# ScalarE in place of VectorE: the first layer's statistics and both FFNs' normalization

## The chip, the core and the metric

The kernel runs on one NeuronCore of one Trainium2 chip. The core has TensorE (PE; PEld are its weight loads), VectorE (DVE), ScalarE (ACT), GpSimd (POOL) and SyncE (SP), each with a queue of instructions that it works off in order; 16 DMA engines move data. The metric is the device time of one execution in microseconds (us), as a median of several. A profile is one further execution, recorded by the hardware profiler.

## The reference

The input x has 16 batches of 512 tokens with 256 features, in float32. Four layers are applied, each on a normalized copy of x (mean 0, variance 1 over the 256 features, no learned factors), and each added to x:

```python
x = x + mamba(layernorm(x))        # a recurrence over the 512 tokens, 16 states per feature
x = x + ffn(layernorm(x))          # "f"
x = x + attention(layernorm(x))    # "a": linear attention, 16 heads of 16
x = x + ffn(layernorm(x))          # "g", same weights as f

def layernorm(x, eps=1e-05):
    m = mean(x, axis=-1); v = var(x, axis=-1)
    return (x - m) / sqrt(v + eps)

def ffn(x): return fp4_linear(silu(fp4_linear(x, w_gate)) * fp4_linear(x, w_up), w_down)
```

`fp4_linear` rounds both of its operands to a 4-bit grid in blocks of 16 along the last dimension, with one scale per block, before it multiplies. The hidden width is 704. Only the two FFNs need the normalized x itself, since it is rounded. In the other two layers the mean is taken out of the weights beforehand, and 1/sqrt(v + eps) is applied while x is transposed.

## The kernel before

**Tiles.** A batch of x stays in one SBUF tile `x` of 128 partitions by 4 chunks by 256 features: a partition holds one token of each chunk. All steps on features are written chunk by chunk, four times per batch.

**Statistics.** There are two ways to get them. The first layer (`front`, lines 435 to 447) uses VectorE: for each chunk `bn_stats` (L442) and `bn_aggr` (L443) give mean and variance, of which only the variance is used. The later layers take the sum of x as a by-product of the residual addition (`residual`, L377, or the halves at L571 added up at L578). `distances` (L384) then lets ScalarE compute the squares of (sum - 256 x), and the accumulator of that instruction gives their sum over the features; the squares themselves go to a scratch tile `squares` that nobody reads. `summed` allots the two small tiles of 128x4, sums and distances, under tags with a number and two buffers each: 0 for f, 1 for g, 2 for a. `inverse` scales the variance and adds epsilon on VectorE (L392) and raises it to the power -0.5 on GpSimd (L394): this gives `rstd`, 128x4, with a tag number of its own (2 for the first layer, 3 for a, 0 and 1 for the FFNs).

**Normalization.** `layernorm` (lines 397 to 409), called by `ffn` alone, calls `inverse`, divides the sums by 256 on VectorE (L402), and then normalizes each chunk by one VectorE instruction (L405) that subtracts the mean and multiplies by rstd, both operands of one value per partition. Its tile `xn` has one buffer per FFN. `fp4` follows on the whole tile of 1024 values per partition: block maxima (L230, `amax`), `half`, `inv`, a product (L244, `v`), an absolute value on ScalarE (L248, `big`), two VectorE instructions that round (L250, L251), and a last product back into `xn` (L252). The tile is then transposed for the matmuls (L418).

**First layer.** `prologue` goes on from `front`: `to_features` lets ScalarE make a diagonal matrix of rstd (L424, `diag_m`) and TensorE multiply x by it (L426), which transposes and scales at once. After projections the scan begins (`mamba`): 16 steps per batch. In each, a DMA spreads the step sizes over the partitions into one of four `bar` buffers (L520), ScalarE makes the decays (L527 exponential, twice, and L530 square), VectorE scans (L548) and multiplies (L552), and TensorE sums up (L558).

**FFN.** For each chunk TensorE computes gate and up (L605), ScalarE a tanh (L611), VectorE two products (L612, L613), and after another `fp4` TensorE transposes (L627), ScalarE copies to SBUF (L631, L636) and TensorE multiplies by w_down (L640).

**Order.** Each stage is a Python generator: it issues some instructions and yields a number, about the microseconds that this piece is to count. `run_all` (from L865 on) starts four stages per batch b, the scan at b, f at b+1.0, attention at b+2.1 and g at b+3.1, and always lets the stage go on that stands earliest. A stage advances by yield times length over total, and the totals are a line of constants:

```python
    SCAN, FFN, ATTN = 65.7, 40.2, 25.7
```

So a scan of batch b runs beside f of b-1, attention of b-2 and g of b-3. Within the scan of batch b, `weave` mixes in the prologue of batch b+1, one piece of it after each scan step from the second on. The yields in `front` are 2.4 after the statistics and 1 after `to_features`; in `ffn` 2.2 follows `layernorm` and 7 follows its `fp4`. The order in which the code issues instructions gives them their priority. The framework's scheduler settles each engine's queue when the kernel is built, and an instruction whose operands come early may stand ahead of ones that were issued before it: in the trace, the `bn_stats` of batches 1 to 4 start at 19, 53, 55 and 57 us, and the first scan step at 62 us.

Of the kernel before, what the change touches and what calls it, by code (L numbers as in the profile page):

```python
# [10 lines left out]
F32 = mybir.dt.float32  # L11
BF16 = mybir.dt.bfloat16
AF = mybir.ActivationFunctionType
ALU = mybir.AluOpType
# [3 lines left out]
P = 128  # L18
# [14 lines left out]
def kernel(  # L33
# [18 lines left out]
    nc = tc.nc  # L52
    B, S, D = x.shape
# [5 lines left out]
    NC = S // P  # L59
# [27 lines left out]
    small = ctx.enter_context(tc.tile_pool(name="small", bufs=2))  # L87
# [9 lines left out]
    begun, turned, stats, halfway = {}, {}, {}, [0]  # L97
# [21 lines left out]
    squares = const.tile([P, D], BF16, name="squares")  # L119
# [248 lines left out]
    def summed(i, name):  # L368

        sums = small.tile([P, NC], F32, tag=f"sum{i}", name=f"sum_{name}")  # L370
        dist = small.tile([P, NC], F32, tag=f"dist{i}", name=f"dist_{name}")
        return sums, dist
# [10 lines left out]
    def distances(xt, c, sums, dist):  # L383
        nc.scalar.activation(  # L384
            squares, xt[:, c, :], AF.Square, bias=sums[:, c : c + 1], scale=-float(D),
            accum_out=dist[:, c : c + 1],
        )

    def inverse(i, var, by, name):

        shifted = small.tile([P, NC], F32, tag=f"var{i}", name=f"var_{name}")
        nc.vector.tensor_scalar(shifted, var, by, LN_EPS, ALU.mult, ALU.add)  # L392
        rstd = small.tile([P, NC], F32, tag=f"rstd{i}", name=f"rstd_{name}")
        nc.gpsimd.tensor_tensor(rstd, shifted, neg_half, ALU.pow)  # L394
        return rstd

    def layernorm(i, xt, stats, name):

        sums, dist = stats
        rstd = inverse(i, dist, 1.0 / D**3, name)  # L400
        mean = small.tile([P, NC], F32, tag=f"mean{i}", name=f"mean_{name}")
        nc.vector.tensor_scalar(mean, sums, 1.0 / D, None, ALU.mult)  # L402
        xn = acts[i].tile([P, NC, D], F32, tag="xn", name=f"xn_{name}", bufs=1)
        for c in range(NC):
            nc.vector.tensor_scalar(  # L405
                xn[:, c, :], xt[:, c, :], mean[:, c : c + 1], rstd[:, c : c + 1],
                ALU.subtract, ALU.mult,
            )
        return xn

    def to_features(pool, t, name, rstd=None):

        tT = pool.tile([P, ND, S], F32, tag="tT", name=f"tT_{name}", bufs=1)
        if rstd is None:
            for k in range(ND):
                pt = bank(f"pt_{name}_{k}")
                for c in range(NC):
                    nc.tensor.transpose(pt[:, ts(c, P)], t[:, c, ts(k, P)], ident)  # L418
                nc.scalar.copy(tT[:, k, :], pt)
            return tT  # L420
        pts = [bank(f"pt_{name}_{k}") for k in range(ND)]
        for c in range(NC):
            diag = small.tile([P, P], F32, tag="diag", name=f"diag_{name}_{c}")
            nc.scalar.activation(diag, ident, AF.Copy, scale=rstd[:, c : c + 1])  # L424
            for k in range(ND):
                nc.tensor.matmul(  # L426
                    pts[k][:, ts(c, P)], t[:, c, ts(k, P)], diag, start=True, stop=True
                )
        for k in range(ND):
            nc.scalar.copy(tT[:, k, :], pts[k])  # L430
        return tT
# [2 lines left out]

    def front(b, xt):

        stats = small.tile(
            [P, NC, nc.vector.BN_STATS_DIM], F32, tag="stats", name=f"st_m{b}"
        )
        mv = small.tile([P, NC, nc.vector.BN_AGGR_DIM], F32, tag="mv", name=f"mv_m{b}")  # L440
        for c in range(NC):
            nc.vector.bn_stats(stats[:, c, :], xt[:, c, :])  # L442
            nc.vector.bn_aggr(mv[:, c, :], stats[:, c, :])  # L443
        rstd = inverse(2, mv[:, :, 1], 1.0, f"m{b}")
        yield 2.4
        turned[b] = to_features(one, xt, f"m{b}", rstd)
        yield 1

    def prologue(b, xt):

        yield from front(b, xt)
        xnT = turned.pop(b)

# [129 lines left out]
    def ffn(i, nm, b, xs):  # L583
        xt = xs[b]
        act = acts[i]
        xq = layernorm(i, xt, stats.pop((nm, b)), f"{nm}{b}")
        if i == 0:
            stats["a", b] = summed(2, f"a{b}")
# [271 lines left out]
        nc.sync.dma_start(out[b].rearrange("(c p) d -> p c d", p=P), xs[b])  # L860


    SCAN, FFN, ATTN = 65.7, 40.2, 25.7

    def run_all(stages):  # L865

# [62 lines left out]
```

## Time and profile before

| | |
|---|---|
| runs | 2825.38 us median of 3 (2824.58 to 2828.75) |
| the profiled execution, its own time | 2823.49 us |
| its span, first to last instruction | 2821.8 us |
| mean granted TensorE clock | 0.942 of full |
| HBM traffic | 146.02 MB read, 16.78 MB written, 58 GB/s over the span |
| from 500 to 2480 us | PE busy 1779.00, DVE 1786.84, ACT 1093.81 of 1980.00 us |
| from 2480 us to the end | PE busy 287.32, DVE 211.69, ACT 96.24 of 341.80 us |

How to read the profile's lines: an instruction group has its line in the kernel, its engine and operation, the tile it writes and those it reads (`out<-in`, buffer numbers left out; the letter at the end of a name is the layer: m first layer, f and g the FFNs, a attention), the shapes as partitions by elements, and how often it occurred. In the rows by form there follow the busy time in us and the mean duration of one in ns, then the idle time of the engine just before, in us, and what ended it. In a timeline the first number is the start in us from the span's start, the second how long the row took, and brackets give idle time before it and who ended it; instructions of the same kind in a row are merged and counted with x. Durations of neighbours on an engine overlap somewhat. In the table by stretch of time each engine has its busy time and the number of instructions, in the order PE, PEld, DVE, ACT, POOL, and at the end the granted clock, the DMA share and GB/s. The chain of waits is followed back from the last instruction, at each step to what released it.

Here is how the same two stages stand in the whole: VectorE executes 64 `bn_stats`, 64 `bn_aggr`, 32 means and 128 normalizations in an execution; ScalarE executes 192 squares with accumulators.

### The profile page before, as it was taken

The page shows a single profiled execution, that of the slowest core. Times are in us where ns is not written, and L with a number is a line of the kernel's source. Part 1 is how long each engine was busy: PE and PEld are TensorE (multiplying, and loading weights), DVE is VectorE, ACT ScalarE, POOL GpSimd, SP SyncE. Part 2 cuts the span into 40 slices and gives each one's busy share as a digit, 9 for nine tenths or more (in the row PEclk, how much of TensorE's full clock was granted, in tenths as well). Part 3 has the DMA queues.
Part 4 walks back from the last instruction along what each step waited for, and adds up shares of the span by engine and source line. Part 5 has one row for each costly group of instructions (what it writes and reads, how often), then busy time and mean ns, then how long its engine had stood idle before and what let it go on. Part 6 is the DMA issues. An engine that isn't in the chain of part 4 may idle for free.

```text
span 2821.8 us, 34272 instructions
## 1 busy us (share of the span) xinstructions
PE 2449.7 (87%) x12907; PEld 1441.9 (51%) x12907; DVE 2430.5 (86%) x3689; ACT 1492.1 (53%) x2846; POOL 172.2 (6%) x171
## 2 busy tenths in 40 slices
PE   5677989799898989989898998989899898889886
PEld 3234545455555555555555555555555554556564
DVE  7898888898999898899989889998988999868465
ACT  4776564465646455464645556464555646333321
POOL 2000000000000010000001000000100000000000
PEclk7788999899999999999999999999999999999897
DMA  5533212222223131322313132131213213000000
GB/s 142 131 93 82 64 49 53 67 53 83 52 60 76 38 75 45 82 53 54 82 38 75 45 82 53 47 89 38 75 45 83 53 45 82 24 8 1 8 8 8
DMA packets 97146, 165.01 MB, mean 58 GB/s; under 512 B 8434, under 2 KB 92372, under 8 KB 96980
## 3 DMA queue, kind: packets, MB, share of 16 engines
q1 hardware_dynamic: 95360, 161.77, 22.3%
q8 instruction: 101, 1.65, 0.3%
q10 hardware_dynamic: 1620, 1.06, 0.1%
q14 instruction: 65, 0.53, 0.1%
HBM read 146.02 MB, written 16.78 MB: 58 GB/s over the span
## 4 chain that ended last, share of the span: by engine, by line
DVE 40%; PE 36%; DMA 9%; ACT 9%; issue 3%; POOL 2%; SPq 0%; POOLq 0%; ACTq 0%; DVEq 0%
DVE h L548 15%; DMA bar<-dd 9%; PE pg_g L605 5%; DVE h L552 4%; PE pu_g L605 4%; PE po_g L640 4%; PE pg_f L605 3%; PE pu_f L605 3%; PE py L558 3%; ACT bar L527 2%; PE pz L457 2%; DVE v_f L244 2%; DVE sm L729 2%; PE pqk L678 2%; ACT bar L530 1%
## 5 line engine op out<-in xcount | busy, mean ns | idle before, releaser
L548 DVE TENSOR_TENSOR_SCAN h<-bar,inp 128x1024 f32<-128x1024 f32 x256 | 579.4, 2277 | 13.9 <-PE py L558 7.6
L527 ACT ACTIVATE bar<-bar,a_col 128x511 f32<-128x511 f32 x512 | 352.4, 715 | 339.6 <-DMA bar<-dd 291.5
L558 PE MATMUL py<-h,red 128*32 128x512 f32 x1024 | 288.7, 645 | 119.3 <-DVE h L552 118.2
L552 DVE TENSOR_TENSOR h<-h,cm 128x1024 f32<-128x1024 f32 x256 | 311.1, 1218 | 0.6
L530 ACT ACTIVATE bar<-bar 128x1022 f32<-128x1022 f32 x256 | 269.3, 1052 | 3.0
L640 PE MATMUL po_g<-wdT,hqT_g 128*128 128x256 f32 (+1 forms) x768 | 214.3, 425 | 41.8 <-ACT hqT_g L631 41.8
L640 PEld LDWEIGHTS po_g<-wdT,hqT_g 128*128 128x128 f32 (+1 forms) x768 | 149.0, 206 | 120.3 <-ACT hqT_g L631 65.1
L640 PE MATMUL po_f<-wdT,hqT_f 128*128 128x256 f32 (+1 forms) x768 | 198.2, 400 | 9.6 <-ACT hqT_f L631 9.6
L605 PE MATMUL pg_g<-wgT,tT_g 128*128 128x352 f32 x512 | 190.7, 492 | 0.3 <-DVE sm L729 0.3
L640 PEld LDWEIGHTS po_f<-wdT,hqT_f 128*128 128x128 f32 (+1 forms) x768 | 137.5, 192 | 94.6 <-ACT hqT_f L636 29.0
L605 PE MATMUL pu_g<-wuT,tT_g 128*128 128x352 f32 x512 | 182.3, 480 | 0.0
L605 PE MATMUL pg_f<-wgT,tT_f 128*128 128x352 f32 x512 | 181.8, 478 | 0.0
L605 PE MATMUL pu_f<-wuT,tT_f 128*128 128x352 f32 x512 | 172.7, 460 | 3.4 <-DVE sm L729 3.0
L729 DVE TENSOR_TENSOR sm<-psc,causal 128x512 f32<-128x512 f32 x256 | 163.9, 681 | 10.8 <-PE psc L722 5.9
L611 ACT ACTIVATE h_g<-pg_g 128x352 f32<-128x352 f32 x128 | 59.1, 462 | 195.3 <-PE pg_g L605 195.1
L558 PEld LDWEIGHTS py<-h,red 128*32 128x32 f32 x1024 | 37.8, 110 | 221.6 <-DVE h L552 171.4
L605 PEld LDWEIGHTS pu_g<-wuT,tT_g 128*128 128x128 f32 x512 | 103.3, 202 | 60.7 <-issue 11.4
L763 POOL COPY dx<-den 128x256 f32<-128x256 f32 x64 | 42.2, 660 | 1482.7 <-PE pr L768 795.5
L248 ACT ACTIVATE big_f<-v_f 128x704 bf16<-128x704 f32 (+1 forms) x80 | 67.2, 840 | 122.3 <-DVE v_f L244 122.3
L605 PEld LDWEIGHTS pg_f<-wgT,tT_f 128*128 128x128 f32 x512 | 96.3, 196 | 66.9 <-issue 23.2
L612 DVE SCALAR_TENSOR_TENSOR h_g<-h_g,pg_g 128x352 f32<-128x352 f32 x128 | 65.5, 512 | 74.2 <-ACT h_g L611 72.8
L678 PE MATMUL pqk<-tT_a,w_qkv_sb 128*128 128x512 f32 x256 | 121.6, 614 | 7.4 <-ACT tT_a L430 7.4
(237 smaller groups left out, 4707.0 us busy)
## 6 DMA issues: line engine op xcount, KB each, us to landing
bar<-dd SPq DMA_DIRECT2D x256, 511.0 KB, 4.7
x<-in_L_attn_a_x_dram SPq DMA_DIRECT2D x16, 512.0 KB, 4.5
dd<-dt SPq DMA_DIRECT2D x128, 64.0 KB, 1.7
out_dram<-x SPq DMA_DIRECT2D x16, 512.0 KB, 4.4
w_qkv_sb<-in_L_attn_b_W_attn_dram ACTq DMA_DIRECT2D x1, 768.0 KB, 7.1
raw_d<-in_L_ffn_w_down_dram SPq DMA_DIRECT2D x1, 704.0 KB
raw_g<-in_L_ffn_w_gate_dram SPq DMA_DIRECT2D x1, 640.0 KB, 7.1
raw_u<-in_L_ffn_w_up_dram SPq DMA_DIRECT2D x1, 640.0 KB, 6.5
```

Of the source, the lines that this page charges most:

```text
L248: nc.scalar.activation(big, v, AF.Abs, scale=STEP)
L527: nc.scalar.activation(bar[:, i, 1:S], bar[:, i, 1:S], AF.Exp, scale=a_col[:, g : g + 1])
L530: nc.scalar.activation(bar[:, :, 1:S], bar[:, :, 1:S], AF.Square)
L548: nc.vector.tensor_tensor_scan(h.rearrange("p i t -> p (i t)"), bar.rearrange("p i t -> p (i t)"), inp.rearrange("p i t -> p (i t)"), 0.0, ...
L552: nc.vector.tensor_tensor(h, h, cm.unsqueeze(1).to_broadcast([P, 2, S]), ALU.mult)
L558: nc.tensor.matmul(py[32 * q : 32 * q + 32, :], red[:, j, :], (h0, h)[q // 2][:, q % 2, :], start=False, stop=(j == 3),)
L605: nc.tensor.matmul(pw[:, :HF], xqT[:, k, ts(c, P)], wT[:, k, cols], start=(k == 0), stop=(k == ND - 1),)
L611: nc.scalar.activation(hc, pg[:, :HF], AF.Tanh, scale=0.5)
L612: nc.vector.scalar_tensor_tensor(hc, hc, 1.0, pg[:, :HF], ALU.add, ALU.mult)
L640: nc.tensor.matmul(po[:, :D], hqT[:rows, r, :], wdT[:rows, r, :], start=(r == 0), stop=(r == NR - 1),)
L678: nc.tensor.matmul(pz, w_qkv_sb[:, k, ts(je, P)], xnT[:, k, :], start=(k == 0), stop=(k == ND - 1),)
L729: nc.vector.tensor_tensor(t, psc[g].rearrange("p (s t) -> p s t", t=P), causal.unsqueeze(1).to_broadcast([P, NH // 4, P]), ALU.mult,)
```

## The change

In `layernorm` the VectorE instruction for the mean becomes one for a shift, -mean times rstd, which needs rstd. The four VectorE normalizations become four ScalarE activations of the function Identity, which compute x times scale plus bias, with rstd as scale and the shift as bias. In `front` the eight VectorE instructions for statistics become eight on ScalarE: for each chunk a Copy whose accumulator gives the sum, and `distances`, which reads that sum. Both write their full result to `squares`. The small tiles come from `summed(0, ...)`, whose two tags the first FFN also uses. The yield after the statistics is 0.2 in place of 2.4, and the scan's total is 63.5 in place of 65.7. The yields and the total of the FFN stay.

```diff
@@ layernorm
         rstd = inverse(i, dist, 1.0 / D**3, name)
-        mean = small.tile([P, NC], F32, tag=f"mean{i}", name=f"mean_{name}")
-        nc.vector.tensor_scalar(mean, sums, 1.0 / D, None, ALU.mult)
+        shift = small.tile([P, NC], F32, tag=f"mean{i}", name=f"shift_{name}")
+        nc.vector.scalar_tensor_tensor(shift, sums, -1.0 / D, rstd, ALU.mult, ALU.mult)
         xn = acts[i].tile([P, NC, D], F32, tag="xn", name=f"xn_{name}", bufs=1)
         for c in range(NC):
-            nc.vector.tensor_scalar(
-                xn[:, c, :], xt[:, c, :], mean[:, c : c + 1], rstd[:, c : c + 1],
-                ALU.subtract, ALU.mult,
+            nc.scalar.activation(
+                xn[:, c, :], xt[:, c, :], AF.Identity, bias=shift[:, c : c + 1],
+                scale=rstd[:, c : c + 1],
             )
@@ front
-        stats = small.tile(
-            [P, NC, nc.vector.BN_STATS_DIM], F32, tag="stats", name=f"st_m{b}"
-        )
-        mv = small.tile([P, NC, nc.vector.BN_AGGR_DIM], F32, tag="mv", name=f"mv_m{b}")
+        sums, dist = summed(0, f"m{b}")
         for c in range(NC):
-            nc.vector.bn_stats(stats[:, c, :], xt[:, c, :])
-            nc.vector.bn_aggr(mv[:, c, :], stats[:, c, :])
-        rstd = inverse(2, mv[:, :, 1], 1.0, f"m{b}")
-        yield 2.4
+            nc.scalar.activation(squares, xt[:, c, :], AF.Copy, accum_out=sums[:, c : c + 1])
+            distances(xt, c, sums, dist)
+        rstd = inverse(2, dist, 1.0 / D**3, f"m{b}")
+        yield 0.2
         turned[b] = to_features(one, xt, f"m{b}", rstd)
         yield 1
@@ the stages' totals
-    SCAN, FFN, ATTN = 65.7, 40.2, 25.7
+    SCAN, FFN, ATTN = 63.5, 40.2, 25.7
```

## The prediction, made before the change was run

> **What bounds the kernel now.** I read the page's shares first, then busy time by stretch, then the timelines of VectorE (DVE) and ScalarE (ACT) where the moved steps sit, then the rows by form. From the page:
>
> ```profile
> PE 2449.7 (87%) x12907; PEld 1441.9 (51%) x12907; DVE 2430.5 (86%) x3689; ACT 1492.1 (53%) x2846; POOL 172.2 (6%) x171
> ...
> DVE 40%; PE 36%; DMA 9%; ACT 9%; issue 3%; POOL 2%; SPq 0%; POOLq 0%; ACTq 0%; DVEq 0%
> ```
>
> Two engines are nearly full, and neither carries the end alone: 40% of the span is followed back to VectorE, 36% to TensorE, 9% to ScalarE. Busy time by stretch (columns: PE, PEld, DVE, ACT, POOL):
>
> ```profile
> 1037.00:1044.00 7.00, 6.91 (x30) 3.97 (x30) 7.00 (x13) 4.93 (x16) 1.35 (x1) 1.00 0.33 85
> 1044.00:1052.00 8.00, 4.01 (x17) 2.25 (x14) 7.29 (x21) 6.98 (x14) 2.90 (x3) 1.00 0.25 57
> 1052.00:1060.00 8.00, 7.42 (x25) 3.77 (x24) 8.00 (x8) 3.16 (x8) 0.58 (x1) 0.79 0.12 34
> ```
>
> The timelines repeat every 165 us per batch from the fourth batch on: four VectorE normalizations in a row start at 880.27, 1044.60 and 1209.89. A batch's head, some 33 us from 1037 on, holds the first FFN's normalization, the second FFN's (of an older batch) and the attention's start together. There VectorE is full (32.25 of 33 us), but from 1044 to 1052 ScalarE is at 6.98 of 8 too. VectorE, then ScalarE, in that stretch one batch later:
>
> ```profile
> 1209.89 1.38 DVE L405 TENSOR_SCALAR xn_f<-x,mean_f,rstd_f 128x256 f32<-128x256 f32 x4 [0.56 <-POOL rstd_f L394]
> ...
> 1211.33 1.21 DVE L230 TENSOR_REDUCE amax_f<-xn_f 128x64 f32<-128x1024 f32 x1
> ...
> 1217.26 1.22 DVE L250 SCALAR_TENSOR_TENSOR v_f<-big_f,v_f 128x1024 f32<-128x1024 bf16 x1 [0.26 <-ACT big_f L248]
> ```
>
> ```profile
> 1210.23 1.33 ACT L527 ACTIVATE bar<-bar,a_col 128x511 f32<-128x511 f32 x2
> 1212.43 0.72 ACT L527 ACTIVATE bar<-bar,a_col 128x511 f32<-128x511 f32 x1 [0.86 <-DMA bar<-dd]
> ...
> 1216.19 1.04 ACT L248 ACTIVATE big_f<-v_f 128x1024 bf16<-128x1024 f32 x1
> ```
>
> VectorE goes from normalizing straight to the block maximum, and is already kept waiting (0.26 us here, 0.51 in another batch) by ScalarE's `big_f`. So the moved work leaves a full engine for one that is nearly full just there.
>
> **What VectorE loses.** Rows by form:
>
> ```profile
> L384 ACT ACTIVATE squares<-x,sum_g 128x256 bf16<-128x256 f32 x64 | 32.3, 505 | 21.8 <-DVE x L377 20.8
> L715 ACT ACTIVATE ko<-qk,odd_heads 128x256 f32<-128x256 f32 x64 | 30.8, 501 | 25.3 <-DVE qk L686 21.5 <-PE psc L722 3.8
> L442 DVE BATCH_NORM_STATS2 st_m<-x 128x6 f32<-128x256 f32 x64 | 24.3, 398 | 0.1
> L405 DVE TENSOR_SCALAR xn_g<-x,mean_g,rstd_g 128x256 f32<-128x256 f32 x64 | 24.2, 392 | 3.7 <-POOL rstd_g L394 3.7
> ```
>
> Instructions overlap, so a duration overstates what an engine gets back. Four normalizations take 1.38 us with a last one of 0.41: one per (1.38-0.41)/3 = 0.323 us. Eight per batch: 2.6 us; 128 in all: 41 us. Two bn_stats in a row take 0.71 us with one of 0.39, so 0.32 each, and their bn_aggr adds 0.09 before the next starts (1020.57 to 1020.65): 0.41 per pair, 1.65 us per batch, 26 us in all. Together 4.25 us per batch, 67 us. The shift replaces the mean at the same size (128x4): L402 takes 0.14 to 0.17 us; I take no difference, bounded by 0 and +0.1 us, as it multiplies by a second operand. The variance step on 128x4 stays. Busy time falls by more, as durations count there: 46.7 (L405) + 24.3 + 10.1 = 81 us, to about 2350.
>
> **What ScalarE gains.** The squares of one batch start 0.635 us apart (1203.76, 1204.39, 1205.03), read-out of the accumulator included. The new Copy with a sum has no row; bounds are 0.46 (a plain 256-wide copy of 0.37 plus 0.09 for the read-out's tail) and 0.635 (the square). I take 0.56, nearer the square, which also reads SBUF and its accumulator. [...] So (0.56+0.635+0.03)x4 = 4.9 us per batch (4.4 to 5.2). For an Identity with both scale and bias per partition the trace has no row: L715 (scale) and L384 (bias) have one such operand and take 0.50. [...] I take 0.49: 2.06 us for four (1.7 to 2.4), 4.1 per batch. ScalarE gains 9.0 us per batch, 144 us in all; its busy time goes to about 1640. No activation table is added that I can see: Copy and Square already run among the others without a load beside them, and Identity, which is not in the trace, costs 1.28 us per load if it is otherwise (the L472 load's row), up to twice per normalization.
>
> [...]
>
> **Where it lies on the path.** First the statistics. At 1019 to 1022 bn_stats are followed by this VectorE row:
>
> ```profile
> 1027.25 0.52 DVE L612 SCALAR_TENSOR_TENSOR h_f<-h_f,pg_f 128x352 f32<-128x352 f32 x1 [3.53 <-ACT h_f L611]
> ```
>
> VectorE idles until ScalarE has done a tanh, which comes after decays that waited for a transfer. Taking 1.65 us away ahead of that wait gains about nothing there. ScalarE's 4.9 us burst is emitted before the fourth step's decay, and ScalarE stood still there for 4.18 us, waiting on that DMA. If it goes into that hole it costs about 0.2 us (what sticks out, less slack); behind the wait it would push the tanh by up to 4.9. The first result is needed 35 us later (var_m at 1022.4, `diag_m` at 1057), so the variance's and POOL's power's delay is hidden. For batch 0 the power on POOL runs only at 18.5 us, behind its other powers; five microseconds on ScalarE are hidden by that. If batch 0's rstd came late, it would cost up to 3 us once. The yield from 2.4 to 0.2 and SCAN from 65.7 to 63.5 let the rest of the prologue be issued earlier against the other stages, by 2.2/65.7 of 165 us = 5 us; issue order, no work. I value it at zero, bounded by -0.5 and +1 us per batch, since a changed order can change every wait of the period.
>
> The normalizations: VectorE saves 2.6 us per batch where it is full. Against it: (1) the shift waits for POOL as the first normalization did (0.56), but then `amax_f` waits 0.16 + 2.06 + hand-overs, some 2.3 us. Behind it VectorE has the g variance, a residual (0.34) and a scan product (1.14), about 1.6 us, ready: 0.7 uncovered. (2) `xn_g` is covered by f's maximum, reciprocal and product (2.7 us). (3) 4.1 us on ScalarE come ahead of `big_f`: 1209.9 to 1217.2 is 7.3 us with 0.86 idle, so `big_f` ends 3.3 us later; VectorE by then has removed 2.6 us but can bring forward `amax_g`, `half_g`, `inv_g` and a scan (4.0 us). Between 0 and 3.2 us remain; I take 0.7, nearer zero, as the order on a queue is already not the order of the code (bn_stats of batches 1 to 4 run before the first scan). Per batch: -2.6 + 0.7 + 0.7 + 0.2 = -1.0 us; thirteen batches have both in full stretches: -13. Four normalizations (f of batch 15, g of 13, 14, 15) stand in the tail, where VectorE has 212 of 342 us and waits: 1.38 becomes 0.16+2.06+0.2, +1.0 each: +4. Sum -9 us.
>
> A check by shares: VectorE's 40% of 2822 us over 2430 busy is 0.46 us of span per us; ScalarE's 9% over 1492 is 0.17. -67x0.46 + 144x0.17 = -31 + 24 = -7. The two agree. From the profiled execution, 2823.5 (span 2821.8), I get 2814.5; it lies 1.9 below the median of the runs, so 2816.
>
> **Rivals.**
> 1. VectorE's whole saving counts: -67x0.85 (the share outside start and tail) + 4 = -53: 2772. For it: VectorE full in the heads. Against: 36% of the chain is TensorE's, whose work stays. Chance 0.10.
> 2. Slower: ScalarE late at `big_f` in the batch head. If VectorE's order leaves nothing before `v_f` L250, it waits 3.2 us instead of 0.7: +1.5 per batch, x13 + 4 = +24: 2849. It decides from 1.7 us of added wait on. For it: ScalarE at 6.98 of 8 and VectorE already waiting; against: 4 us of movable work. Chance 0.40, the disturbed issue order included.
> 3. Nothing reaches the end, TensorE or bar transfers take the relief: 2825. Chance 0.12.
>
> **How the numbers follow.** A small gain (0.38; own range 2795 to 2819) and rival 1 make 0.48 for faster by over 0.2% (5.7 us, about what a measurement of this kernel can tell from no change), 0.12 within, 0.40 slower. The range reaches up past rival 2 to 2858 and down near rival 1, to 2778.
>
> **What would show it.** DVE near 2350 and ACT near 1640 busy; the period between normalizations 164 us; `amax_f` waiting for ScalarE's `xn_f` under 1 us, `v_f` L250 for `big_f` about 1 us. A wait of over 1.7 us there, or `h_f` waits above 3.5 us, would make rival 2 right. New table loads, or a normalization of over 2.4 us, would make the prices wrong; so would a period that changes while those waits stay.

## The result, and the profile after

The changed kernel takes 2866.34 us in the median of 4 runs (2859.41 to 2869.59), the kernel before 2826.86 (4 runs, 2824.58 to 2828.75): a ratio of 1.0137, 95% interval 1.0116 to 1.0158. It is slower by 39 us, where 9 us of gain were predicted, and lies outside of the predicted range of 2778 to 2858. The profiled execution took 2865.66 us, its span is 2863.9, its mean granted TensorE clock 0.929 (before: 0.942).

From the page after, shares of the engines and then the chain that ended last:

```profile
PE 2442.8 (85%) x12907; PEld 1449.6 (51%) x12907; DVE 2369.5 (83%) x3433; ACT 1600.3 (56%) x3230; POOL 194.3 (7%) x171
...
PE 31%; DVE 30%; ACT 21%; DMA 10%; POOL 4%; issue 4%; SPq 0%; POOLq 0%; ACTq 0%; DVEq 0%
```

VectorE lost 61 us of busy time and ScalarE got 108, yet VectorE's share fell from 86 to 83% of a longer span: it is more often idle. Lines behind 445 have numbers 3 lower than before. The rows by form of what was moved, and of the waits behind it (busy, mean ns of one, idle before and its releaser):

```profile
L405 ACT ACTIVATE xn_f<-x,shift_f,rstd_f 128x256 f32<-128x256 f32 x64 | 33.3, 590 | 15.1 <-DVE shift_f L402 15.1
...
L439 ACT ACTIVATE squares<-x 128x256 bf16<-128x256 f32 x64 | 25.8, 403 | 1.1 <-DMA x<-in_L_attn_a_x_dram 1.0
...
L250 DVE SCALAR_TENSOR_TENSOR v_f<-big_f,v_f 128x1024 f32<-128x1024 bf16 x16 | 19.5, 1219 | 11.5 <-ACT big_f L248 11.5
L230 DVE TENSOR_REDUCE amax_f<-xn_f 128x64 f32<-128x1024 f32 x16 | 19.4, 1215 | 0.6 <-ACT xn_f L405 0.4
...
L402 DVE SCALAR_TENSOR_TENSOR shift_f<-sum_f,rstd_f 128x4 f32<-128x4 f32 x16 | 2.6, 163 | 14.5 <-POOL rstd_f L394 14.5
```

One Identity with two operands takes 590 ns, four in a row 2.07 us (2.06 predicted). The two waits that the prediction watched are small: `amax_f` waited 0.4 us for ScalarE in all, `v_f` 11.5/16 = 0.7 us per batch. The head of a batch before, and then the changed kernel's: GpSimd's power of f and VectorE's rows behind it, and then ScalarE's:

```profile
1042.65 1.91 POOL L394 TENSOR_TENSOR rstd_f<-var_f,neg_half 128x4 f32<-128x4 f32 x1 [13.79 <-DVE var_f L392]
...
1046.04 1.21 DVE L230 TENSOR_REDUCE amax_f<-xn_f 128x64 f32<-128x1024 f32 x1
```

```profile
1063.10 1.91 POOL L394 TENSOR_TENSOR rstd_f<-var_f,neg_half 128x4 f32<-128x4 f32 x1 [15.20 <-DVE var_f L392]
...
1065.05 0.17 DVE L402 SCALAR_TENSOR_TENSOR shift_f<-sum_f,rstd_f 128x4 f32<-128x4 f32 x1 [0.90 <-POOL rstd_f L394]
...
1065.19 2.29 DVE L545 TENSOR_TENSOR_SCAN h<-bar,inp 128x1024 f32<-128x1024 f32 x1
1068.31 0.16 DVE L402 SCALAR_TENSOR_TENSOR shift_g<-sum_g,rstd_g 128x4 f32<-128x4 f32 x1 [0.83 <-POOL rstd_g L394]
1068.39 2.28 DVE L545 TENSOR_TENSOR_SCAN h<-bar,inp 128x1024 f32<-128x1024 f32 x1
...
1070.92 1.21 DVE L230 TENSOR_REDUCE amax_f<-xn_f 128x64 f32<-128x1024 f32 x1
```

```profile
1065.24 2.07 ACT L405 ACTIVATE xn_f<-x,shift_f,rstd_f 128x256 f32<-128x256 f32 x4 [0.60 <-DVE shift_f L402]
...
1073.08 0.40 ACT L439 ACTIVATE squares<-x 128x256 bf16<-128x256 f32 x1
...
1078.96 1.04 ACT L248 ACTIVATE big_f<-v_f 128x1024 bf16<-128x1024 f32 x1
```

`amax_f` need not wait, since two whole scans stand ahead of it: it starts 7.8 us after GpSimd's power of f, before 3.4. And the first layer's statistics, which were to fill a hole near 1019, run at 1073 to 1081, in this head.

From the fifth power of f to the fifteenth, f recurs every 170.3 us; before, every 165.0: these ten periods lose 53 us. The stretch ahead of them loses 11 more (724.5 against 713.4 us), and the stretch behind them wins 22 back (437 against 459 us, 5 of it after the last scan): 42 us of span in all. So most of the loss is the 5.3 us of each steady period, and the question is what in the period carries it.

### The profile page after: what moved, and what is told of

Its sections match the earlier page's. It is cut to its first block, busy times and chain, and to the rows that moved or that the text cites. A ratio compares the mean times of both kernels' runs of the same rounds, so it can differ in the third digit from the quotient of the medians.

```text
span 2863.9 us, 34409 instructions
## 1 busy us (share of the span) xinstructions
PE 2442.8 (85%) x12907; PEld 1449.6 (51%) x12907; DVE 2369.5 (83%) x3433; ACT 1600.3 (56%) x3230; POOL 194.3 (7%) x171
## 4 chain that ended last, share of the span: by engine, by line
PE 31%; DVE 30%; ACT 21%; DMA 10%; POOL 4%; issue 4%; SPq 0%; POOLq 0%; ACTq 0%; DVEq 0%
DVE h L545 13%; DMA bar<-dd 10%; PE po_g L637 7%; ACT bar L524 4%; ACT bar L527 3%; PE pg_g L602 3%; PE py L555 3%; PE pu_g L602 3%; DVE h L549 2%; PE pg_f L602 2%; PE pu_f L602 2%; POOL rstd_g L394 1%; ACT big_f L248 1%; DVE amax_f L230 1%; PE pn L750 1%
## 5 line engine op out<-in xcount | busy, mean ns | idle before, releaser
L555 PE MATMUL py<-h,red 128*32 128x512 f32 x1024 | 262.7, 658 | 148.6 <-DVE h L549 148.5
L637 PE MATMUL po_g<-wdT,hqT_g 128*128 128x256 f32 (+1 forms) x768 | 248.1, 477 | 81.2 <-ACT hqT_g L628 81.2
L637 PEld LDWEIGHTS po_g<-wdT,hqT_g 128*128 128x128 f32 (+1 forms) x768 | 171.1, 236 | 178.0 <-ACT hqT_g L628 113.6
L637 PE MATMUL po_f<-wdT,hqT_f 128*128 128x256 f32 (+1 forms) x768 | 197.7, 399 | 14.7 <-ACT hqT_f L628 14.7
L602 PE MATMUL pg_g<-wgT,tT_g 128*128 128x352 f32 x512 | 183.8, 482 | 11.4 <-ACT dt L464 7.5
L726 DVE TENSOR_TENSOR sm<-psc,causal 128x512 f32<-128x512 f32 x256 | 163.9, 682 | 28.7 <-PE pn L750 22.7
L555 PEld LDWEIGHTS py<-h,red 128*32 128x32 f32 x1024 | 34.7, 111 | 254.3 <-DVE h L549 208.1
L760 POOL COPY dx<-den 128x256 f32<-128x256 f32 x64 | 32.1, 502 | 1778.5 <-PE pr L765 1236.7
L609 DVE SCALAR_TENSOR_TENSOR h_f<-h_f,pg_f 128x352 f32<-128x352 f32 x128 | 65.7, 514 | 86.6 <-ACT h_f L608 86.6
L602 PEld LDWEIGHTS pu_f<-wuT,tT_f 128*128 128x128 f32 x512 | 97.0, 191 | 61.6 <-DVE x L377 8.4
```

The source lines that it names most:

```text
L555: nc.tensor.matmul(py[32 * q : 32 * q + 32, :], red[:, j, :], (h0, h)[q // 2][:, q % 2, :], start=False, stop=(j == 3),)
L602: nc.tensor.matmul(pw[:, :HF], xqT[:, k, ts(c, P)], wT[:, k, cols], start=(k == 0), stop=(k == ND - 1),)
L609: nc.vector.scalar_tensor_tensor(hc, hc, 1.0, pg[:, :HF], ALU.add, ALU.mult)
L637: nc.tensor.matmul(po[:, :D], hqT[:rows, r, :], wdT[:rows, r, :], start=(r == 0), stop=(r == NR - 1),)
L726: nc.vector.tensor_tensor(t, psc[g].rearrange("p (s t) -> p s t", t=P), causal.unsqueeze(1).to_broadcast([P, NH // 4, P]), ALU.mult,)
L760: nc.gpsimd.tensor_copy(dx, den[:, c * NH : (c + 1) * NH].unsqueeze(2).to_broadcast([P, NH, HD]))
```

## Experiments

Each ratio is to the kernel before, run beside it on the same chip; before's own median was 2815.64 us beside the first four, then, group by group, 2823.84, 2822.94, 2830.70 and (the last two runs) 2835.00. The theories:

- *load* (in the last group *work*): the work added to ScalarE, and the longer way through it, costs the time in any order.
- *tag*: the first layer's statistics share a tag with f's and so come late, into the head.
- *turn*: VectorE waits at the two shifts for GpSimd, lets whole scans in, and f's blocks come late.
- *order*: in the first group this said that the changed numbers by themselves bring the loss. From the third group on (there called *settle*) it says that every edit lets the build settle the queues of all engines in another way, and which way decides, not the work.

**The change in parts.** `norm_only` has the normalization on ScalarE alone (L402 and L405 of the diff). `front_only` has the statistics on ScalarE with the two numbers of the change. `order_only` has these two numbers and moves no step. `own_tag` is the whole change with tiles of its own for the statistics:

```diff
# order_only, against before
-        yield 2.4
+        yield 0.2
-    SCAN, FFN, ATTN = 65.7, 40.2, 25.7
+    SCAN, FFN, ATTN = 63.5, 40.2, 25.7
# own_tag, against the changed kernel
-        sums, dist = summed(0, f"m{b}")
+        sums, dist = summed(3, f"m{b}")
```

> Only the normalization moves to ScalarE (shift and four Identity activations); statistics, yields and totals stay as before. If the shared tags of the statistics are the cause (theory tag), this part is nearly free: 2815 to 2835 us. If it is ScalarE's added work in the batch head, whichever it is (theory load), this part carries about half of the loss: 2840 to 2855 us. If the changed issue order is the cause (theory order), 2815 to 2830 us.

> Only the first layer's statistics move to ScalarE, with the yield of 0.2 and the total of 63.5; the normalization stays on VectorE. Theory tag: the statistics of a batch again run in the batch head behind the f sums of two batches earlier, and most of the loss is here: 2850 to 2870 us. Theory load: about half of the loss, 2840 to 2855 us. Theory order: nearly all of it, 2855 to 2870 us.

> No step moves; only the yield after the statistics is 0.2 in place of 2.4 and the scan's total 63.5 in place of 65.7. Theory order: it carries most of the loss, 2850 to 2870 us. Theories tag and load: 2820 to 2835 us.

> The whole change, but the first layer's sums and distances have small tiles under tags of their own (number 3 in place of 0). Theory tag: the statistics run when x has arrived, some 40 us before the batch head, and most of the loss of 39 us goes: 2820 to 2840 us. Theory load: the same work is on ScalarE, so 2855 to 2870 us. Theory order: the order numbers are unchanged, 2855 to 2870 us.

Measured: norm_only 2878.33 us, ratio 1.0224 (1.0196 to 1.0252); front_only 2815.15, 1.0001 (0.9987 to 1.0015); order_only 2784.40, 0.9894 (0.9872 to 0.9916); own_tag 2860.81, 1.0168 (1.0143 to 1.0193). With its own tag the statistics still ran in the head: VectorE's and ScalarE's instructions follow each other as in the changed kernel from the first to the last (3433 and 3230), and the period is the same (170.4 and 170.3 us). So *tag* fell. The normalization looked guilty. But two numbers that move no work gained 31 us, where the prediction had put zero, and *order* as it stood had put the loss. Three of the four times lie outside of what any theory had expected; own_tag lies where *load* and *order* had it.

**Inside the normalization.** `norm_f` and `norm_g` have only one FFN's on ScalarE (a branch on `i`). `extra_act` is before with the eight Identity activations added, written to the scratch tile. `shift_dve` keeps the normalization on VectorE, but as x*rstd + shift, so that it waits for GpSimd as in the change:

```diff
# extra_act, at the end of layernorm
+        for c in range(NC):
+            nc.scalar.activation(
+                squares, xt[:, c, :], AF.Identity, bias=mean[:, c : c + 1],
+                scale=rstd[:, c : c + 1],
+            )
# shift_dve: shift in place of mean, as in the change, and
-                xn[:, c, :], xt[:, c, :], mean[:, c : c + 1], rstd[:, c : c + 1],
-                ALU.subtract, ALU.mult,
+                xn[:, c, :], xt[:, c, :], rstd[:, c : c + 1], shift[:, c : c + 1],
+                ALU.mult, ALU.add,
```

> Only the first FFN (f) is normalized by ScalarE; the second stays on VectorE, statistics, yields and totals as before. Normalizing both cost 2.2%, 63 us. Theory turn (the way from rstd over ScalarE and back to the block maximum is longer, VectorE fills the hole with whole scans and f starts late): most of the 63 us is here, +35 to +60 us, since f takes the whole period of a batch. Theory load (ScalarE's added time): half of it, +20 to +40 us.

> Only the second FFN (g) is normalized by ScalarE. Theory turn: little, -10 to +15 us but for the tail, since g has slack within the period. Theory load: the other half, +20 to +40 us.

> VectorE normalizes as before, and ScalarE makes the same eight Identity activations per batch besides, into the scratch tile that nobody reads (added work, nothing taken out). Theory load: +30 to +60 us, as ScalarE has the same 4 us per batch more at the same place and VectorE gets nothing back. Theory turn: -5 to +15 us, as nobody waits for these results.

> VectorE normalizes, but with the shift: it waits for rstd at the shift and computes x times rstd plus shift. No work moves. Theory turn: within 10 us of before, since the waiting instruction is only one earlier and VectorE itself goes on. If waiting for GpSimd at the shift is what costs, +20 us or more.

Measured: norm_f 2820.78, 0.9989 (0.9968 to 1.0010); norm_g 2784.14, 0.9859 (0.9828 to 0.9889); extra_act 2860.63, 1.0130 (1.0096 to 1.0163); shift_dve 2840.33, 1.0061 (1.0037 to 1.0086). One FFN costs nothing, the other gains 1.4%, both together lose 2.2%: the parts do not add. In norm_f neither *turn* nor *load* has what it expected. extra_act spoke for *load*; shift_dve lost 16 us, between the two cases of its expectation.

**Turn against order.** `shift_pool` is norm_only with the shift made by GpSimd, so that VectorE has no wait there. `norm_order` and `g_order` are norm_only and norm_g with the numbers 0.2 and 63.5. `yield_only` is before with 0.2 but SCAN left at 65.7.

```diff
# shift_pool, against norm_only
-        nc.vector.scalar_tensor_tensor(shift, sums, -1.0 / D, rstd, ALU.mult, ALU.mult)
+        nc.vector.tensor_scalar(sums, sums, -1.0 / D, None, ALU.mult)
+        nc.gpsimd.tensor_tensor(shift, sums, rstd, ALU.mult)
```

> The whole normalization on ScalarE as in norm_only (2.2% over before), but the shift is made by GpSimd right after its power, so that VectorE no longer waits for GpSimd at shift_f and shift_g (14.5 us each in the changed kernel); sums is scaled by VectorE ahead of that. ScalarE has the same work as in norm_only. Theory turn (VectorE's waits at the two shifts, with a scan of 2.3 us let in behind each, make f's blocks late): amax_f comes back from 7.8 to about 5 us after rstd_f, the period falls from 170.5 to about 165 us, time within 0.5% of before (2810 to 2840). Theory load (ScalarE's 4.7 us per batch of Identity is itself what costs): nothing comes back, 2865 to 2890. Theory settle (the queues come out differently with every edit, and no single wait carries it): anything between, and amax_f's place does not go with the time.

> norm_only with the two planner numbers of the change (yield 0.2, SCAN 63.5); the statistics of the front stay on VectorE. It is the corner that is missing between before, order_only (-1.1%), norm_only (+2.2%), front_only (0.0%) and the changed kernel (+1.4%). If effects add, norm_only's +2.2% and order_only's -1.1% give +1.1%, about 2855. Theory load: the numbers help here as they do alone, 2850 to 2860. Theory turn: the head's queue is that of norm_only whatever the numbers are, the period stays near 170 us and the time at 2865 to 2885. Theory settle: it does not add up, either way, by more than 0.5%.

> norm_g (only the FFN of g is normalized on ScalarE, -1.4% alone) with the two planner numbers (-1.1% alone). If the two gains were separate pieces of time, they would add: -2.5%, about 2755. Theory settle (each is one lucky settling of the same queues): they don't add, 2770 to 2830. Theory turn says nothing against adding, since g's shift lies behind f's blocks in the queue: about 2760.

> Before with the yield after the front's statistics at 0.2 and SCAN left at 65.7, so that the scan's steps are issued over a period that is 2.2 units too long for them: an issue order that nobody has any use for, and no step moved. Theory settle: its time differs from before and from order_only by 0.5 to 1.5%, in either direction. If order_only's gain was that of the earlier transposes alone, this has most of it too: 2780 to 2800. If the order of issue hardly matters: within 0.3% of before.

Measured: shift_pool 2854.33, 1.0124 (1.0083 to 1.0164); norm_order 2769.93, 0.9817 (0.9786 to 0.9847); g_order 2851.42, 1.0099 (1.0066 to 1.0132); yield_only 2870.82, 1.0169 (1.0116 to 1.0222). In shift_pool `amax_f` came back to 5.7 us after the power, as *turn* expected, but not the time; g_order lies above all that was expected of it. norm_order decides. It has the work of norm_only, and the same head; VectorE's timeline of norm_only, then of norm_order:

```profile
1068.94 0.16 DVE L402 SCALAR_TENSOR_TENSOR shift_f<-sum_f,rstd_f 128x4 f32<-128x4 f32 x1 [0.90 <-POOL rstd_f L394]
...
1074.82 1.22 DVE L230 TENSOR_REDUCE amax_f<-xn_f 128x64 f32<-128x1024 f32 x1
...
1085.81 1.22 DVE L250 SCALAR_TENSOR_TENSOR v_f<-big_f,v_f 128x1024 f32<-128x1024 bf16 x1 [0.77 <-ACT big_f L248]
```

```profile
1035.05 0.16 DVE L402 SCALAR_TENSOR_TENSOR shift_f<-sum_f,rstd_f 128x4 f32<-128x4 f32 x1 [0.90 <-POOL rstd_f L394]
...
1040.93 1.21 DVE L230 TENSOR_REDUCE amax_f<-xn_f 128x64 f32<-128x1024 f32 x1
...
1051.86 1.23 DVE L250 SCALAR_TENSOR_TENSOR v_f<-big_f,v_f 128x1024 f32<-128x1024 bf16 x1 [0.72 <-ACT big_f L248]
```

From `shift_f` to `amax_f` it is 5.88 us in both, to `v_f` 16.87 and 16.81. All that *turn* spoke of is there in both, and one is 4% quicker than the other: 0.9817/1.0224 = 0.960. *Turn* fell, at least as what decides. Nor does `amax_f`'s place go with the time elsewhere: it starts 3.4 us after the power in order_only (-1.1%) and in extra_act (+1.3%), 7.8 in norm_order (-1.8%) and in after_ffn of the next group (+2.6%). One period of norm_only in three stretches, and then one of norm_order (columns: PE, PEld, DVE, ACT, POOL, then clock, DMA share, GB/s):

```profile
1067.00:1097.00 30.00, 24.65 (x97) 12.81 (x97) 26.45 (x31) 23.75 (x47) 6.74 (x3) 0.89 0.28 67
1097.00:1137.00 40.00, 38.08 (x170) 23.76 (x169) 39.63 (x63) 28.76 (x47) 0.40 (x1) 0.96 0.21 53
1137.00:1237.10 100.10, 88.33 (x538) 53.45 (x536) 80.46 (x126) 42.55 (x91) 3.73 (x5) 0.95 0.22 58
```

```profile
1033.00:1063.00 30.00, 24.11 (x96) 12.55 (x92) 26.50 (x32) 23.34 (x48) 6.74 (x3) 0.89 0.25 68
1063.00:1103.00 40.00, 39.06 (x173) 24.52 (x172) 39.79 (x65) 29.82 (x49) 0.40 (x1) 1.00 0.22 53
1103.00:1198.70 95.70, 86.23 (x541) 51.35 (x539) 80.41 (x127) 42.73 (x92) 5.41 (x6) 0.96 0.24 62
```

The first 30 us hold the head, alike to 0.05 us of VectorE. The next 40 differ little. In the rest VectorE does the same, 80.46 and 80.41 us of work, but in 100.1 and in 95.7 us. So here the loss lies far behind the steps that were moved, as idle time. In the mean of ten periods, summed from the trace, VectorE is idle for 3.3 us of the first 30 in norm_only and 3.2 in norm_order, and afterwards for 20.0 and 13.7. It is spread over many waits; the largest single difference makes 1.3 of the 6.3 us. And the queues differ there. The same 220 VectorE instructions make a period in both, in an order that hardly changes from period to period within a run, but only 183 of them stand in a common order. On TensorE, for one, norm_order has a projection of the prologue (L496) ahead of the FFN's gate matmul (L605), and norm_only behind it.

Another order can lose its time elsewhere. In yield_only, which moves no step, VectorE's added idle time is in the head (6.7 of the first 30 us, before 1.0; afterwards 14.7 and 15.1), nearly all of it at one line of the attention. The line's row before, and then in yield_only:

```profile
L686 DVE SCALAR_TENSOR_TENSOR qk<-ep 128x512 f32<-128x512 f32 x64 | 43.6, 682 | 16.5 <-ACT ep L685 16.1
```

```profile
L686 DVE SCALAR_TENSOR_TENSOR qk<-ep 128x512 f32<-128x512 f32 x64 | 43.9, 686 | 96.9 <-ACT ep L685 96.9
```

**The whole work in other orders.** `after_old_numbers` is the changed kernel with before's numbers (2.4 and 65.7), `after_half` the same half-way (1.3 and 64.6). `after_ffn`, `before_ffn` and `norm_order_ffn` change another pair, as the change did for the scan:

```diff
-        yield 2.2
+        yield 0.2
         fp4(act, xq.rearrange("p c d -> p (c d)"), NC * D, nm)
-    SCAN, FFN, ATTN = 63.5, 40.2, 25.7
+    SCAN, FFN, ATTN = 63.5, 38.2, 25.7
```

`front_old_numbers` has the statistics alone on ScalarE, with before's numbers.

> The changed kernel's work (statistics of the front and both normalizations on ScalarE) with before's planner numbers, yield 2.4 and SCAN 65.7. Theory work: 2850 to 2885. Theory order: no telling where, but more than 1% away from 2866 in either direction with even odds; it fills the last corner of the square of moved work and numbers.

> The changed kernel, all its work as it is, with one more planner number: the yield after the FFN's normalization is 0.2 instead of 2.2, and the FFN's total 38.2 instead of 40.2 (the same consistent pair as the change made for the scan). Theory work (ScalarE's added work and the longer way through it cost 1.4% in any order): 2850 to 2885, within 0.7% of the changed kernel. Theory order (the loss belongs to the order in which the change was built, not to its work): the time leaves the changed kernel's 2866 by more than 1%, most likely downward, to 2770 to 2835.

> Before with the FFN's yield after the normalization at 0.2 and its total at 38.2, no step moved. Theory order: another time than before by 0.5 to 2%, sign unknown, as order_only (-1.1%) and yield_only (+1.7%) had. Theory work: within 0.5% of before, about 2825.

> norm_order (both normalizations on ScalarE, statistics on VectorE, yield 0.2 and SCAN 63.5: -1.8%, the quickest so far) with the FFN's numbers as in after_ffn. Theory order: it leaves norm_order's 2770 by about 1% or more, upward rather than downward since norm_order is at the low end of all orders seen: 2775 to 2850. If the FFN's numbers help by themselves, 2740 to 2770.

> The changed kernel's whole work with planner numbers half-way between before's and its own: yield 1.3 and SCAN 64.6 (before's numbers gave -1.1%, its own +1.4%). If the time follows the numbers smoothly: +0.2%, between -0.3 and +0.7%. Theory order (each order settles by itself): outside of that band with two chances in three, in either direction.

> Only the front's statistics on ScalarE, with before's planner numbers (yield 2.4, SCAN 65.7); with the changed numbers it was front_only, 0.0%. If the prediction's step on the statistics holds by itself (VectorE 1.65 us per batch less, ScalarE's part hidden): -0.4 to -1.0%, 2800 to 2818. Theory order: anything from -1.8 to +2.6%, the span of the orders seen.

Measured: after_old_numbers 2800.17, 0.9890 (0.9868 to 0.9912); after_ffn 2902.97, 1.0260 (1.0227 to 1.0292); before_ffn 2879.49, 1.0174 (1.0150 to 1.0198); norm_order_ffn 2818.57, 0.9959 (0.9947 to 0.9971); after_half 2851.76, 1.0070 (1.0048 to 1.0091); front_old_numbers 2851.56, 1.0060 (1.0043 to 1.0077). The changed kernel's whole work with before's numbers is quicker than before; with its own it is slower. after_ffn and before_ffn moved by more than 1%, as *order* expected, but after_ffn upward, where downward was thought likelier. front_old_numbers missed what the prediction's own step would give (-0.4 to -1.0%). Busy time from 500 to 2480 us, the changed kernel's row and then that of after_old_numbers:

```profile
500.00:2480.00 1980.00, 1739.10 (x9367) 1036.62 (x9366) 1694.61 (x2464) 1154.07 (x2329) 138.40 (x105) 0.94 0.23 59
```

```profile
500.00:2480.00 1980.00, 1776.61 (x9699) 1066.17 (x9698) 1752.88 (x2559) 1173.33 (x2373) 151.52 (x108) 0.96 0.24 60
```

In the same time after_old_numbers gets through 2559 VectorE instructions in place of 2464; its f recurs every 163.9 us (alternating 159 and 169), the changed kernel's every 170.3. VectorE's head is that of the changed kernel here too, up to `v_f`, but for a scan and a product that change places in every second period: of the first 30 us it is idle for 3.4 (3.6 in the changed kernel), of the rest of a period for 15.0 (21.2).

Two of the parts could be on or off with either pair of numbers. The table has the changes against before, in per cent:

| on ScalarE | numbers 2.4, 65.7 | numbers 0.2, 63.5 |
|---|---|---|
| nothing | 0 (before) | -1.1 (order_only) |
| statistics | +0.6 (front_old_numbers) | 0.0 (front_only) |
| normalization | +2.2 (norm_only) | -1.8 (norm_order) |
| both | -1.1 (after_old_numbers) | +1.4 (the changed kernel) |

Moving the normalization is worth +2.2, -1.7, -0.7 or +1.4, depending on the two others: +0.3 on average. Moving the statistics: +0.6, -3.3, +1.1, +1.4-(-1.8) = +3.2; +0.4 on average. The numbers: -1.1, -0.6, -4.0, +2.5; -0.8 on average. Both moves together are worth -1.1 with the old numbers and +2.5 with the new ones. No part has a price of its own that is large beside this scatter; one of a few tenths of a per cent could not be seen in it. The half-way numbers gave +0.7 between -1.1 and +1.4, at the edge of what a smooth slope would give, so that a slope is neither shown nor excluded.

norm_order is the version that beats both: 2769.93 against 2822.94 us before on its chip, ratio 0.9817.

## Why the prediction was wrong

**The step that failed** is the value of the changed issue order: "I value it at zero, bounded by -0.5 and +1 us per batch". With no step moved the new numbers gave -31 us (order_only), 31/16 = 1.9 us per batch (in the trace about half of it lies in the ten steady periods, 2.1 us each, and half behind them); with the change's whole work they cost 1.0137/0.9890 = 2.5%, some 70 us, and 170.3-163.9 = 6.4 us per steady period, six times the upper bound. The sentence named the danger, "a changed order can change every wait of the period", and then bounded it by a number no row gave.

One period in two stretches, before and then the changed kernel, and below it VectorE's mean over ten periods, in us:

```profile
1042.65:1072.65 30.00, 24.80 (x112) 14.07 (x112) 29.25 (x40) 22.99 (x46) 4.83 (x3) 0.94 0.24 61
1072.65:1207.94 135.29, 125.31 (x692) 75.16 (x691) 119.82 (x190) 69.17 (x133) 5.35 (x7) 0.96 0.25 62
```

```profile
1063.10:1093.10 30.00, 22.80 (x95) 12.28 (x92) 26.46 (x31) 24.00 (x58) 8.64 (x4) 0.89 0.21 58
1093.10:1232.63 139.53, 125.82 (x710) 75.91 (x710) 118.90 (x183) 74.99 (x145) 3.39 (x5) 0.96 0.23 60
```

| VectorE, per period | before | changed | after_old_numbers |
|---|---|---|---|
| busy | 148.8 | 145.5 | 145.5 |
| idle, first 30 us from f's power on | 1.0 | 3.6 | 3.4 |
| idle, rest | 15.1 | 21.2 | 15.0 |
| period | 165.0 | 170.3 | 163.9 |

The work saved (3.3 us) and the waits added in the head (2.6 us) nearly cancel, and the prediction had reckoned with both (2.6 saved and 1.6 added per batch). What it put at zero is the rest of the period, 6.1 us of idle time behind the head, and with before's numbers this is gone. That after_old_numbers' period falls by 1.1 us, near the predicted 1.0, confirms nothing: its queues are not those of before either.

**Behind it stands the sum itself.** It followed the moved instructions through the queues of before, with every other instruction left in its place. But the edits settled the queues anew (own_tag left those of VectorE and ScalarE as they were), also 70 to 160 us behind the moved steps. That is why terms which were about right, or wrong by little, did not add up to the result:

- *Prices*. The Identity held: four in 2.07 us (2.06), 0.590 for one. The 0.49 us from one Identity to the next, and the 0.03 in the sum for the statistics, were the author's estimates, which no row of before shows. The statistics were priced too high: the Copy with a sum holds ScalarE for 0.40 us until the next instruction starts (1079.91 to 1080.31), where 0.56 was taken, the square 0.51 (1080.77 to 1081.28) instead of 0.635. That is 3.6 us per batch, not 4.9, and about half of why ScalarE's busy time came to 1600.3 and not 1640. VectorE's came to 2369.5, not 2350: it fell by 61 us, near the 67 counted from start to start and not the 81 counted by durations, which overlap. Table loads stayed at 32, of 1.28 us each.
- *Statistics*, placed wrongly: in the head, not in the hole. But after_old_numbers has them there and is quick, so that this is not the loss.
- *The waits in the head*, near in sum for the wrong reason. `amax_f` and `v_f` wait 0.4/16 and 0.7 us per batch (0.7 taken for each). What was not seen is that both shifts wait for GpSimd (14.5/16 = 0.9 us each, where the normalizations had waited 0.7 and 0.2) and that two scans pass `amax_f`. norm_order has all of it and is 1.8% quicker than before.
- *The share check* confirmed nothing. Its rates (0.46 us per us of VectorE, 0.17 of ScalarE) came from a chain that belongs to one order: in the changed kernel the chain gives VectorE 30% and ScalarE 21%, and in order_only, with before's work, 35 and 12%.

**Rival 2** had the sign without its cause: it decides from 1.7 us of added wait at `v_f`, and the whole wait is 0.7. Its chance of 0.40 held "the disturbed issue order included"; that clause was the result, and deserved a case of its own. **The last sentence** of what would show the prices wrong, "a period that changes while those waits stay", is what came, though the prices were not the reason: it was a sign of the order.

**What stays open.** Which property of an order makes the period 163 or 170 us, or 175.5 as in after_ffn, was not found. The slow ones (norm_only, yield_only, before_ffn, front_old_numbers, the changed kernel: 170.1 to 170.7) have different VectorE and ScalarE work, and their waits lie in different places, as norm_only and yield_only show. An edit may also move tiles in memory, and no run separates that from the order; the one that gave tiles of their own, own_tag, kept the order of VectorE and ScalarE and the period. A run with the work of one kernel and the queues of another, instruction by instruction, would be the clean test; it was not tried.

## What to carry to other kernels

Where two engines are nearly full and a build settles the queues, a shift of 1% is within the reach of the issue order alone: here eighteen edits gave -1.8 to +2.6%, and two kernels with the same work lay up to 4% apart. Before a step is called cheap or dear, run its control (the order changed, no work moved) and run the step in two or three orders; otherwise one measures the draw. And a forecast from local waits needs a range at least as wide as such a control scatters, with the order as a rival of its own.

## What the runs showed of the hardware

In the heads of norm_only and of the changed kernel TensorE's granted clock is lower behind a pause. Two stretches of 5 us in norm_only, from 5 us after f's power on (the number behind the five engines is the granted clock):

```profile
1072.00:1077.00 5.00, 0.03 (x2) 0.00 (x0) 4.78 (x7) 2.60 (x6) 0.99 (x2) 0.86 0.66 146
1077.00:1082.00 5.00, 4.70 (x14) 2.53 (x15) 4.70 (x8) 2.89 (x8) 1.11 (x1) 0.50 0.28 67
```

TensorE stands still for 5 us (busy for 0.03), and in the next 5 us its granted clock is 0.50. In the changed kernel's head four `py` matmuls (L555) take 1.05 us ahead of the pause (from 1066.61 us on, clock 1.00) and 1.92 us behind it (from 1073.39 on, clock 0.50), with TensorE idle for 5.72 us between them. The four take 0.87 us longer behind the pause; that every pause costs time in this way was not shown. From 500 to 2480 us the granted clock is 0.94 in the changed kernel and 0.96 in after_old_numbers. An estimate from these two numbers and the 1739.10 us of PE busy time there, taken to grow as the clock falls: some (0.96-0.94)/0.96 of it, 36 us over 11.6 periods, or 3 us each of the 6.4, if all of it reached the end. The pause in the head is in the quick norm_order as well (no matmul from 1038.1 to 1043.1 us, then a clock of 0.50 for 5 us), and in the two periods shown above TensorE's busy time differs by only 1.7 us (151.06 against 149.40 in sum). No run separates the clock's part from the rest, or shows how much of it is a cause of the longer period and how much a result.
